# Layer 1's Gram matrices and weight products at the start of a two-layer decoder, layer 0's feed forward in the second part

## The chip, the cores and the metric

The kernel is one program on one core of a Trainium2 chip. The core has five engines that run their own instruction streams: TensorE (PE, matmuls, with weight loads shown as PEld), VectorE (DVE), ScalarE (ACT), GpSimd (POOL) and SyncE (SP, which here issues every DMA). The metric is device microseconds of one execution, the median of several runs. Before the change it is 2391.16 us (three runs, 2387.3 to 2392.27).

## What is computed

The input is 64 sequences of 64 tokens with 256 features, 4096 tokens in all, and a context of the same shape. Six blocks follow one another, each adding to x what it makes of the layer norm of x:

```
x = x + L0_attn(ln(x))          # 16 query heads of 128, 4 key/value heads, layer norm of q and k, rotary, causal
x = x + L0_xattn(ln(x), ctx)    # 8 channels a head; softmax over the 256 features of ctx; no weights
x = x + L0_ffn(ln(x))           # base 256x256, plus the rank-16 correction of the one expert (of 8) that the router picks
x = x + L1_attn(ln(x))          # 16 heads of 16, one key/value head, causal
x = x + L1_xattn(ln(x), ctx)    # 16 heads of 128; q and k with an RMS norm over all 2048 features; output 2048 -> 256
x = x + L1_ffn(ln(x))           # 704 wide, weights and activations quantized to 8 bits
```

Layer 1's cross attention needs two things of its weights alone. The RMS norm of x @ q_w + q_b over 2048 features is a quadratic form in x, so the kernel computes the Gram matrix of [q_w, q_b] (256 x 257, a sum over 2048 features), and the same for ki. And the value and output weights of each head are multiplied into one 256 x 256 matrix a head (the weight products).

## The kernel before

Tokens go in 16 groups of 256. A group's first part (attention a0, cross attention x0 and feed forward f0 of layer 0) ends with a store of x to DRAM ("mid"); its second part (a1, x1, f1 of layer 1) begins with the load. All sixteen first parts come before most of the second parts, as the weights of layer 0 and of layer 1 don't fit beside each other: a pool of 67 buffers of 2 KB a partition ("k2") holds 20 pieces of layer 0's weights and later 32 pieces of layer 1's.

Matmuls in full precision are made of three 16-bit matmuls (high x high, high x low, low x high), in the helper mm3 (lines 412 to 414); some are plain fp32.

No loop runs in the order in which it is written. Each step (a few instructions on one engine) is an Op with an estimated cost, the buffers it reads and writes, an earliest start (tmin) and a due time. A planner (Sched.plan) runs once when the program is built: it takes, again and again, the step that can start first; among steps that can start within EPS ns of each other it takes the one with the earliest due time. What it decides is each engine's instruction order, which the chip then follows strictly, with semaphores for the dependences. The due time is the group's base (PACE), plus the step's place in its group, plus a constant for each kind of step (the table LEAD). At most five groups are in flight (WINDOW). PSUM has eight banks (class "B"), which all stages share.

Setup work has no group. Layer 0's weights are loaded, centred, scaled by a power of two and split into two 16-bit parts (split_weight, lines 475 to 531). The scale of the context (ctx_scale) and layer 0's remaining setups follow with earliest starts of 30 to 70 us, among them l0_ffn_setup and l1_attn_setup. Layer 1's cross attention setup (l1_xattn_setup, line 1426) and feed forward setup have an earliest start of 150 us and more. In it:

- gram_setup (line 1326), once for q and once for ki: eight loads of 128 x 2 x 257 fp32; for each load and each half h of the 256 rows two fp32 matmuls into a fresh PSUM bank g_ps (line 1343), for h = 0 also one-column matmuls that sum the squares of the bias (line 1345), and an addition of the bank to an SBUF tile g_G on DVE (lines 1350 to 1354). STEP[0] = 15 us lie between the earliest starts of two loads.
- value_out_setup (line 1375): eight pairs of loads n_v and n_o, 32 fp32 matmuls into n_ps (line 1392), a copy and a sum of squares on ACT (lines 1395 and 426), a store to DRAM (line 1398); then, when the largest value is known, the products are read again, scaled, split (w_hl) and stored.

l1_xattn_load (line 1484) brings layer 1's prepared weights into k2 buffers. The first three weights wait for the attention of group 14, the other five for that of group 15.

l0_ffn (line 1108): a layer norm, a 16-bit split and a DMA transpose (to_T, line 556); for each half of the group six matmuls of 392 columns into f_ps, a routing chain of small DVE operations (lines 1129 to 1134), a transpose hm_ps, a copy hT, a fp32 matmul f0o_ps (line 1143) and two additions to x (lines 1136 and 1144).

Cross attention of layer 0 works with matmuls on quarters of PE's array (xs_ps line 1009, xt_ps line 1043, xo_ps line 1059), the row maximum on DVE (xmx, line 1016) and the exponential on ACT (line 1050). In layer 1's cross attention the value matrices (vn_ps, line 1511) are the largest single use of PE.

## Time and profile before

| what | value |
|---|---|
| median of 3 runs | 2391.16 us |
| the profiled execution's own time | 2390.41 us |
| its span, first to last instruction | 2388.5 us |
| PE busy | 2169.8 us (91%) |
| weight loads | 1701.9 us (71%) |
| DVE busy | 1948.4 us (82%) |
| ACT busy | 1516.3 us (63%) |
| POOL busy | 1630.4 us (68%) |
| mean granted PE clock | 0.961 |
| moved by DMA | 220.83 MB, 92 GB/s |

The profile is one execution. Busy time is the time in which an engine had at least one instruction running; matmuls overlap each other, so a sum of single durations is larger than the busy time. The page cuts the span into 40 slices of 60 us. "fill" below is busy time divided by the length of a stretch. Idle time of an engine says something about the end only where that engine sets the pace.

### The profile page before, as it was taken

What the parts mean: (1) busy time and instruction counts of PE and PEld (TensorE: products, weight loads), DVE (VectorE), ACT (ScalarE), POOL (GpSimd) and SP (SyncE); (2) the same over time, 40 slices, a digit from 0 to 9 for tenths busy, and PEclk for the clock granted to TensorE, in tenths of its full rate; (3) what the DMA queues carried; (4) which work ended last, traced back from release to release, by engine and by line L of the source; (5) the groups of instructions that cost most, each with busy time, mean ns of one, the idle gap of its engine ahead of it and who ended that gap; (6) DMA issues with size and microseconds to landing.
All of it is one profiled execution on the core that took longest, in us unless ns stands there. A gap on an engine that the chain in (4) does not pass through costs nothing. (4 is left out here: it accounts for less than half of the span.)

```text
span 2388.5 us, 69732 instructions
## 1 busy us (share of the span) xinstructions
PE 2169.8 (91%) x28232; PEld 1701.9 (71%) x28232; DVE 1948.4 (82%) x4532; ACT 1516.3 (63%) x2843; POOL 1630.4 (68%) x1572
## 2 busy tenths in 40 slices
PE   3499999888999898898878999999999999999996
PEld 2387666655566565665544779898999898899995
DVE  7768788898797889898988867887888888888767
ACT  6475666877878676777557565565556565566542
POOL 5899668777787577767645466767777666666632
PEclk9699999999999998999977999999999999999997
DMA  5243234444355333433464353343444334444321
GB/s 182 74 88 91 59 83 107 125 129 103 87 136 136 108 92 83 129 97 80 111 158 108 57 118 72 76 80 73 86 82 80 76 76 81 81 86 77 59 42 28
DMA packets 484323, 220.83 MB, mean 92 GB/s; under 512 B 340568, under 2 KB 463384, under 8 KB 484000
## 3 DMA queue, kind: packets, MB, share of 16 engines
q1 hardware_dynamic: 484000, 216.37, 39.9%
q8 instruction: 222, 3.64, 0.6%
q14 instruction: 101, 0.83, 0.1%
HBM read 89.06 MB, written 34.64 MB: 52 GB/s over the span
## 5 line engine op out<-in xcount | busy, mean ns | idle before, releaser
L1050 ACT ACTIVATE xpt<-xt_ps,xes 128x512 f32<-128x512 f32 x512 | 313.2, 698 | 75.5 <-PE xt_ps L1043 71.7
L1511 PE MATMUL vn_ps<-x1wn,cTs 128*64 128x256 f16 x6144 | 354.1, 274 | 0.0
L1511 PEld LDWEIGHTS <-cTs 128*64 128x64 f16 x6144 | 332.1, 110 | 8.4 <-issue 6.2
L1016 DVE TENSOR_REDUCE xmx<-xs_ps 128x2 f32<-128x512 f32 x512 | 317.2, 679 | 18.1 <-PE xs_ps L1009 17.4
L1518 DVE SCALAR_TENSOR_TENSOR vn<-vn_ps,vn 128x512 f16<-128x512 f32 x256 | 174.5, 684 | 96.9 <-ACT vn L1516 96.4
L1516 ACT ACTIVATE vn<-vn_ps 128x512 f16<-128x512 f32 x256 | 151.9, 595 | 159.3 <-PE vn_ps L1511 157.5
L604 POOL TENSOR_TENSOR s<-s,sm_mx 128x1024 f32<-128x1024 f32 x96 | 184.7, 1924 | 78.8 <-DVE sm_mx L603 71.4
L633 POOL TENSOR_TENSOR phl<-s,phl 128x512 f16<-128x512 f32 x192 | 223.6, 1176 | 12.3 <-ACT phl L632 10.3
L630 POOL TENSOR_TENSOR s<-s,sm_sm 128x512 f32<-128x512 f32 x192 | 199.5, 1056 | 4.7 <-POOL sm_sm L623 0.3
L1059 PE MATMUL xo_ps<-xpt,xve 128*32 128x256 f32 x2048 | 165.0, 414 | 7.1 <-DVE s L1291 4.9
L815 POOL TENSOR_TENSOR qu<-qu,sw 128x512 f32<-128x512 f32 x128 | 165.5, 1304 | 2.0
L813 POOL TENSOR_TENSOR sw<-sw,rp0s 128x512 f32<-128x512 f32 x128 | 165.3, 1304 | 2.2 <-ACT sq L811 1.6
L810 ACT COPY sw<-q_ps 64x512 f32<-64x512 f32 x256 | 148.0, 580 | 28.1 <-PE q_ps L414 18.8
L632 ACT CAST phl<-s 128x512 f16<-128x512 f32 x192 | 118.2, 622 | 73.7 <-POOL s L630 70.8
L1761 POOL TENSOR_TENSOR gu<-gu 128x704 f32<-128x704 f32 x32 | 55.0, 1721 | 138.2 <-ACT sig L1759 129.9
L1620 ACT ACTIVATE k<-qk_ps,x1kb 128x256 f32<-128x256 f32 x242 | 101.4, 471 | 72.6 <-PE qk_ps L414 67.3
L412 PE MATMUL q_ps<-xT,l0w 128*128 128x256 f16 x512 | 139.8, 273 | 3.7 <-ACT sw L810 1.8
L412 PE MATMUL acc<-l0w,ohl 128*128 128x256 f16 x512 | 141.7, 277 | 0.6 <-ACT sw L810 0.2
L413 PE MATMUL acc<-l0w,ohl 128*128 128x256 f16 x512 | 141.4, 276 | 0.0
L414 PE MATMUL acc<-l0w,ohl 128*128 128x256 f16 x512 | 141.3, 276 | 0.0
L412 PE MATMUL qk_ps<-cTs,x1wki 128*128 128x256 f16 x512 | 140.3, 274 | 0.0
L412 PE MATMUL qk_ps<-xT,x1wq 128*128 128x256 f16 x512 | 139.7, 273 | 0.2 <-DVE xmx L1016 0.2
(414 smaller groups left out, 6666.4 us busy)
## 6 DMA issues: line engine op xcount, KB each, us to landing
ovl<-hl_d SPq DMA_DIRECT2D x96, 128.0 KB
vx<-vt SPq DMA_DIRECT2D x64, 128.0 KB
ctx<-in_ctx_dram SPq DMA_DIRECT2D x32, 256.0 KB
hl_d<-hl SPq DMA_DIRECT2D x64, 128.0 KB
wd<-w_hl SPq DMA_DIRECT2D x32, 256.0 KB
q1st<-q_d SPq DMA_DIRECT2D x128, 64.0 KB
xt<-in_x_dram SPq DMA_DIRECT2D x16, 256.0 KB
ctx_a<-in_ctx_dram SPq DMA_DIRECT2D x8, 512.0 KB
```

The lines of the kernel that those rows point to most:

```text
L412: nc.tensor.matmul(out, lh, rh, start=(st and i == 0), stop=False, **kw)
L604: s.o("POOL", 1900, [mx], [s1], lambda m, t: nc.gpsimd.tensor_tensor(t, t, bc(m, 2, 64), ALU.subtract))
L630: s.o("POOL", 1030, [sm], [s1.sub(j)], lambda m, t, h=h: nc.gpsimd.tensor_tensor(t[:, h], t[:, h], bc(m[:, h], 2, 64), ALU.mult))
L633: s.alt([("POOL", c_pool(482), lambda t, _, p, h=h: nc.gpsimd.tensor_tensor(pl(p, 1), t[:, h], pl(p, 0), ALU.subtract)), ("DVE", c_dves(51 ...
L813: s.o("POOL", 1225, [sg], [sw], lambda t, w: nc.gpsimd.tensor_tensor(v(w), v(w), bc(t, 1, 8), ALU.mult))
L815: ("POOL", 1225, lambda w, d: nc.gpsimd.tensor_tensor(view(d), view(d), w, ALU.add))], [sw], [dt])
L1016: nc.vector.tensor_reduce(m[:, h, bs % 4, :], p, AX.X, ALU.max))
L1050: nc.scalar.activation(t, p, AF.Exp, scale=a))
L1059: nc.tensor.matmul(o[32 * hh:32 * hh + 32, hs, :], v[:, n, a:a + 32], r[hh][:, n, :], start=(n == 0 and hs == 0), stop=(n == 1), skip_grou ...
L1511: nc.tensor.matmul(r[-1][64 * h:64 * h + 64, p, :], x[:, b // 2, a, k, t], w.part(r, c, 2 * (2 * p + h) + k), start=(n == 0), stop=(n == 5))
L1516: nc.scalar.activation(v(t), p, AF.Copy, scale=2.0 ** -15))
L1518: nc.vector.scalar_tensor_tensor(v(l), p, 2.0 ** -15, v(h), ALU.mult, ALU.subtract))
```

## The change

Six things change. The Gram matrices accumulate over all eight loads in two PSUM banks; of the second half of the rows only the 129 columns from the diagonal block on are computed, and the sums are copied out (and doubled) once at the end. The products are split off into value_out_products, and both Gram matrices and the products get an earliest start of 5 us with 3 us between loads. Layer 1's self attention setup is called with layer 1's other setups, at 150 us. Layer 0's feed forward becomes the first stage of the second part, so "mid" holds x before it. Layer 1's weights wait for the attention of groups 12, 12, 13, 14 and then 15. The planner's numbers are new: EPS, PEN, LEAD, SPACE, SHIFT, PACE, WINDOW, three costs of PE, HOLD (which puts off a step that changes PE's tiling), a table FINE that shifts single steps of a group, and DVE as an alternative for four memsets.

In the diff the rows of the tables LEAD and FINE are left out:

```diff
--- before.py
+++ after.py
@@ -34,7 +34,7 @@
 WARM = 0.375 * TICK
 LAT = 180
 SWITCH = 96
-HOLD = 0
+HOLD = 55
 DMA_NS = 2300
 SP_NS = 480
 TR_NS = 1240
@@ -224,6 +224,9 @@
             base = g * ii if ph == "a" else ng * PACE["a"][0] + (g - ng) * ii + SHIFT
             for o, t in zip(ops, memo[ph]):
                 o.due += base + t * stretch
+            for i, n, v in FINE[ph]:
+                for o in ops[i:i + n]:
+                    o.due += v
 
     def pe_run(self, st, c, duty):
 
@@ -930,7 +933,8 @@
     two = s.T("k4", [4, 8 * D], F16, name="xtwo")
     s.o("POOL", 1500, [], [two], lambda t: nc.gpsimd.memset(t, 2.0))
     for t in w.q + w.k:
-        s.o("POOL", 2000, [], [t], lambda t: nc.gpsimd.memset(t, 0.0))
+        s.alt([("POOL", 2000, lambda t: nc.gpsimd.memset(t, 0.0)),
+               ("DVE", 1130, lambda t: nc.vector.memset(t, 0.0))], [], [t])
     for t in w.k:
         s.o("SP", DMA_NS, [two], [t], lambda a, t: nc.sync.dma_start(t[3::32].rearrange("p a m -> p (a m)"), a))
 
@@ -1009,7 +1013,7 @@
                         nc.tensor.matmul(p[h][:, mc, :], part(q, h, bs)[:, 128 * mc:128 * mc + 128],
                                          part(k, h, bs), start=True, stop=True)
             s.space = sp
-            s.o("PE", 300, rows, ps, f, duty=0.85, tile=1)
+            s.o("PE", 345, rows, ps, f, duty=0.85, tile=1)
             s.space = None
             for h in range(4):
                 s.o("DVE", c_dve(512), [ps[h]], [mx.sub((bs, h))], lambda p, m, bs=bs, h=h:
@@ -1043,7 +1047,7 @@
                             nc.tensor.matmul(p[h][:, n, :], part(k, h, bs)[:, 128 * n:128 * n + 128],
                                              part(q, h, bs), start=True, stop=True)
                 s.space = sp
-                s.o("PE", 300, [Q.sub(r) for r in (0, 1, 2, ("m", j))] + [K], ps, f, duty=0.85, tile=1)
+                s.o("PE", 325, [Q.sub(r) for r in (0, 1, 2, ("m", j))] + [K], ps, f, duty=0.85, tile=1)
                 s.space = None
                 for h in range(4):
                     s.o("ACT", c_act(512, 1), [ps[h], w.es], [pt[h]], lambda p, a, t:
@@ -1059,7 +1063,7 @@
                             nc.tensor.matmul(o[32 * hh:32 * hh + 32, hs, :], v[:, n, a:a + 32],
                                              r[hh][:, n, :],
                                              start=(n == 0 and hs == 0), stop=(n == 1), skip_group_check=True)
-                s.o("PE", 975, [ve] + pts[hs], [po], f, duty=0.82, tile=2)
+                s.o("PE", 1010, [ve] + pts[hs], [po], f, duty=0.82, tile=2)
             so = s.T("k2", [128, 2, D], name="so")
             s.alt([("ACT", c_act(512), lambda p, t: nc.scalar.copy(t, p)),
                    ("DVE", c_dve(512), lambda p, t: nc.vector.tensor_copy(t, p))], [po], [so])
@@ -1332,36 +1336,31 @@
     g = s.T("k4", [128, 2, 257], name="g_G")
     s.o("POOL", 600, [], [g], lambda t: nc.gpsimd.memset(t, 0.0))
     w.bb = s.fixed(c.tile([128, 1], F32, name=f"bb_{name}"))
+
+    pa, pb = s.T("B", [128, 258], name="g_ps"), s.T("B", [128, 129], name="g_ps")
     for q in range(8):
         t = s.T("k4", [128, 2, 257], name="g_w")
         s.o("SP", DMA_NS + 1500, [], [t], lambda t, q=q: nc.sync.dma_start(t, src[:, 2 * q:2 * q + 2, :]))
-        for h in range(2):
-            ps = s.T("B", [128, 258], name="g_ps")
-
-            def f(t, p, q=q, h=h):
-                for k in range(2):
-                    nc.tensor.matmul(p[:, 0:257], t[:, k, 128 * h:128 * h + 128], t[:, k, :], start=(k == 0), stop=(k == 1))
-                for k in range(2 - 2 * h):
-                    nc.tensor.matmul(p[:, 257:258], t[:, k, 256:257].to_broadcast([128, 128]), t[:, k, 256:257],
-                                     start=(k == 0), stop=(k == 1))
-            s.o("PE", 1108, [t], [ps], f)
-
-            def f(p, g, bb, q=q, h=h):
-                nc.vector.tensor_tensor(g[:, h, :], g[:, h, :], p[:, 0:257], ALU.add)
-                if h == 0 and q == 0:
-                    nc.vector.tensor_copy(bb, p[:, 257:258])
-                elif h == 0:
-                    nc.vector.tensor_tensor(bb, bb, p[:, 257:258], ALU.add)
-            s.o("DVE", 410 - 70 * h, [ps], [g.sub(h)] + ([w.bb] if h == 0 else []),
-                (lambda p, g, bb, f=f: f(p, g, bb)) if h == 0 else (lambda p, g, f=f: f(p, g, None)))
-        s.tmin += STEP[0]
+
+        def f(t, a, b, q=q):
+            for k in range(2):
+                kw = dict(stop=(q == 7 and k == 1), skip_group_check=True)
+                st = q == 0 and k == 0
+                nc.tensor.matmul(a[:, 0:257], t[:, k, 0:128], t[:, k, :], start=st, **kw)
+                nc.tensor.matmul(b, t[:, k, 128:256], t[:, k, 128:257], start=st, **kw)
+                nc.tensor.matmul(a[:, 257:258], t[:, k, 256:257].to_broadcast([128, 128]), t[:, k, 256:257],
+                                 start=False, **kw)
+        s.o("PE", 1600, [t], [pa, pb], f)
+        s.tmin += STEP[2]
     am = s.T("sm", [128, 1], name="g_am")
 
-    def f(g, bb):
-        nc.vector.tensor_scalar(g[:, 0, 128:257], g[:, 0, 128:257], 2.0, None, ALU.mult)
-        nc.vector.tensor_scalar(g[:, 1, 256:257], g[:, 1, 256:257], 2.0, None, ALU.mult)
-        nc.vector.tensor_scalar(bb, bb, 1.0 / 2048, 1e-6, ALU.mult, ALU.add)
-    s.o("DVE", 360, [], [g, w.bb], f)
+    def f(a, b, g, bb):
+        nc.vector.tensor_copy(g[:, 0, 0:128], a[:, 0:128])
+        nc.vector.tensor_scalar(g[:, 0, 128:257], a[:, 128:257], 2.0, None, ALU.mult)
+        nc.vector.tensor_copy(g[:, 1, 128:256], b[:, 0:128])
+        nc.vector.tensor_scalar(g[:, 1, 256:257], b[:, 128:129], 2.0, None, ALU.mult)
+        nc.vector.tensor_scalar(bb, a[:, 257:258], 1.0 / 2048, 1e-6, ALU.mult, ALU.add)
+    s.o("DVE", 850, [pa, pb], [g, w.bb], f)
     square_sum(e, g, am, 514, lambda a: a)
     sc, w.un = pow2_scale(e, am, 14, name)
     w.w = s.fixed(c.tile([128, 2, 2, 257], F16, name=f"gw_{name}"))
@@ -1372,13 +1371,12 @@
     return w
 
 
-def value_out_setup(e, I):
-
+def value_out_products(e, I):
 
     nc, s = e.nc, e.s
     w = e.x1
-    nd = s.fixed(e.dx.tile([4096, D], F32, tag="x1nf", name="nf_d"))
-    am = s.T("sm", [128, 16], name="n_am")
+    nd = w.nd = s.fixed(e.dx.tile([4096, D], F32, tag="x1nf", name="nf_d"))
+    am = w.am = s.fixed(e.cst.tile([128, 16], F32, name="n_am"))
     hv = lambda n, q: I[n].rearrange("(h p) n -> p h n", p=128)[:, 2 * q:2 * q + 2, :]
     for q in range(8):
         v, o = (s.T("k2", [128, 2, D], name="n_" + n) for n in "vo")
@@ -1397,7 +1395,15 @@
             square_sum(e, nf, am.sub(k), 512, lambda a, k=k: a[:, k:k + 1])
             s.o("SP", DMA_NS + 1400, [nf], [nd.sub(k)], lambda t, d, k=k: nc.sync.dma_start(
                 d[D * k:D * k + D].rearrange("(c p) n -> p c n", p=128), t))
-        s.tmin += STEP[0]
+        s.tmin += STEP[2]
+
+
+def value_out_setup(e, I):
+
+
+    nc, s = e.nc, e.s
+    w = e.x1
+    nd, am = w.nd, w.am
     am1 = s.T("sm", [128, 1], name="n_am1")
     s.o("DVE", 75, [am], [am1], lambda a, b: nc.vector.tensor_reduce(b, a, AX.X, ALU.max))
     sc, un = pow2_scale(e, am1, 14, "x1n")
@@ -1432,8 +1438,12 @@
     w.bo, w.i2 = col("bo", 128), col("i2", S)
     s.o("SP", DMA_NS, [], [w.bo], lambda t: nc.sync.dma_start(t, I["bones"]))
     s.o("SP", DMA_NS, [], [w.i2], lambda t: nc.sync.dma_start(t, I["i2"]))
+    t0 = s.tmin
+    s.tmin = STEP[3]
     w.gq = gram_setup(e, I, "gram_q")
     w.gk = gram_setup(e, I, "gram_k")
+    value_out_products(e, I)
+    s.tmin = t0
 
     s.o("DVE", 80, [w.gq.un], [w.gq.us],
         lambda a, t: nc.vector.tensor_scalar(t, a, 1.0 / (2048 * XS), None, ALU.mult))
@@ -1485,7 +1495,7 @@
     nc, s = e.nc, e.s
     order = [("ki", 0), ("q", 0), ("n", 0), ("n", 1), ("ki", 1), ("q", 1), ("n", 2), ("n", 3)]
     for i, (d, u) in enumerate(e.x1.w[k] for k in order):
-        s.after = after[i > 2]
+        s.after = after[i]
         for k, t in enumerate(u.tiles):
             s.o("SP", DMA_NS + 1500, [d], [t], lambda d, u, k=k: nc.sync.dma_start(
                 u, d[:, k // 2, 1024 * (k % 2):1024 * (k % 2) + 1024]))
@@ -1828,55 +1838,82 @@
     e.ctx_sc, e.ctx_un = pow2_scale(e, a1, 10, "ctx")
 
 
-EPS = 41.41
-PEN = 182.83
+EPS = 40.9
+PEN = 155.97
 NQ = 1
 LEAD = {
...
 }
+FINE = dict(a=[
...
 FOLD = [False, True]
-SPACE = (7898, 3165)
+SPACE = (7294, 2944)
 BURST = 1
-SHIFT = 2276.53
+SHIFT = -5805.18
 START = (0, 3e3, 15e3, 22e3, 40e3, 3e3, 30e3, 36e3, 60e3, 70e3)
-PACE = dict(a=(77726.07, 2.1), b=(72833.37, 2.08))
-STEP = (15e3, 60e3)
-WINDOW = (5, 6)
+PACE = dict(a=(74702.12, 2.31), b=(65478.21, 1.96))
+STEP = (15e3, 60e3, 3e3, 5e3)
+WINDOW = (5, 5)
 COUNTS = dict(B=8, k4=6, k2=67, k1=6, sm=10, dram=4)
 SIZE = dict(k8=8192, k4=4096, k2=2048, k1=1024, sm=256)
 
@@ -1901,15 +1938,15 @@
     common_setup(e, I)
 
     e.ovl = s.fixed(e.cst.tile([128, 4096 + 4096 * NQ], F16, name="ovl"))
-    sa = [n for n in stages if n in ("a0", "x0", "f0")]
-    sb = [n for n in stages if n in ("a1", "x1", "f1")]
+    sa = [n for n in stages if n in ("a0", "x0")]
+    sb = [n for n in stages if n in ("f0", "a1", "x1", "f1")]
     if "a0" in sa:
         l0_attn_setup(e, I)
     s.tmin = START[6]
     ctx_scale(e, I, nt)
-    for nm, f in (("x0", l0_xattn_setup), ("f0", l0_ffn_setup), ("a1", l1_attn_setup)):
+    for nm, f in (("x0", l0_xattn_setup), ("f0", l0_ffn_setup)):
         if nm in sa + sb:
-            s.tmin = START[dict(x0=7, f0=8, a1=9)[nm]]
+            s.tmin = START[dict(x0=7, f0=8)[nm]]
             f(e, I)
     s.tmin = 0.0
     mid = {}
@@ -1939,6 +1976,8 @@
         if g == min(1, ng - 1) and sb:
             s.grp = ng - 0.5
             s.tmin = 150e3
+            if "a1" in sb:
+                l1_attn_setup(e, I)
             if "x1" in sb:
                 l1_xattn_setup(e, I)
             if "f1" in sb:
@@ -1949,7 +1988,7 @@
         if not sa and "x1" in sb:
             l1_xattn_setup(e, I)
         if "x1" in sb:
-            l1_xattn_load(e, [e.done.get(("a0", max(g, 0))) for g in (ng - 2, ng - 1)])
+            l1_xattn_load(e, [e.done.get(("a0", max(ng - k, 0))) for k in (4, 4, 3, 2, 1, 1, 1, 1)])
         if "f1" in sb:
             if not sa:
                 l1_ffn_prep(e, I)
```

## The prediction

> **What bounds the kernel now.** I read the page's table of slices first, then busy time by stage, then what TensorE (PE) waits for in each stage, then the rows of the work that the change touches.
>
> The page's 40 slices (60 us each; busy tenths, and the granted clock):
>
> ```profile
> PE   3499999888999898898878999999999999999996
> DVE  7768788898797889898988867887888888888767
> PEclk9699999999999998999977999999999999999997
> DMA  5243234444355333433464353343444334444321
> ```
>
> PE is a third busy in the first two slices, eight to nine tenths until slice 22, and full from slice 23 on but for the last. The same in numbers, by stage (PE, weight loads, DVE, ACT, POOL busy, clock, DMA share, GB/s):
>
> ```profile
> 0.00:120.00 120.00, 50.20 (x399) 36.05 (x400) 89.47 (x228) 63.24 (x125) 86.43 (x95) 0.80 0.42 128
> 120.00:420.00 300.00, 285.47 (x3152) 214.22 (x3149) 241.52 (x577) 198.57 (x353) 243.27 (x213) 0.99 0.37 85
> 420.00:1140.00 720.00, 652.34 (x7469) 443.85 (x7468) 624.56 (x1438) 541.61 (x983) 538.91 (x489) 0.97 0.43 109
> 1140.00:1380.00 240.00, 200.82 (x2293) 124.52 (x2292) 203.70 (x466) 145.49 (x283) 126.86 (x129) 0.86 0.46 105
> 1380.00:2280.00 900.00, 895.24 (x13676) 808.27 (x13676) 713.21 (x1653) 531.15 (x1041) 605.43 (x618) 1.00 0.41 80
> 2280.00:2388.50 108.50, 85.72 (x1258) 74.95 (x1252) 75.98 (x173) 36.21 (x64) 29.44 (x32) 0.88 0.18 33
> 120.00:1380.00 1260.00, 1138.63 (x12909) 782.59 (x12907) 1069.78 (x2479) 885.67 (x1617) 909.05 (x829) 0.96 0.42 103
> ```
>
> PE idles 218.7 us in all: 69.8 before 120 us, 121.4 from 120 to 1380 (fill 1138.63/1260 = 0.904), 4.8 from 1380 to 2280 (fill 0.9947), 22.8 in the tail. So the second part is set by PE alone; the first part is nearly set by it (DVE follows at 0.849, POOL 0.721, ACT 0.703); the start is a chain of weight preparation in which PE has nothing to do. In the first part no single wait owns the idle time. The top of PE's waits from 420 to 1140:
>
> ```profile
> PE mx_ps L1018 <- DVE xmx L1016: 5.5, 8, 1.2
> PE s_ps L911 <- POOL kf L889: 4.6, 2, 4.1
> PE xt_ps L1043 <- DVE s L913: 3.4, 3, 2.7
> ```
>
> The largest is 5.5 of 67.7 us: an order written out beforehand that doesn't fit everywhere. PE work taken out there should therefore shorten the stage at about its fill.
>
> **The change, part by part.** All durations are of the profiled execution: 2390.41 us, span 2388.5; the median of the runs is 2391.16, 0.75 more.
>
> The rows:
>
> ```profile
> L1343 PE MATMUL g_ps<-g_w x128: 377/381/484, 162.8 to 397.6; 128*128 128x257 f32 x128
> L1392 PE MATMUL n_ps<-n_o,n_v x64: 379/379/483, 653.1 to 763.3; 128*128 128x256 f32 x64
> L1114 POOL TENSOR_TENSOR xt<-xt,f0b 128x512 f32<-128x512 f32 x16 | 20.9, 1307 | 23.0 <-DVE xh L547 22.5 <-PE ss_t L870 0.6
> L1143 PE MATMUL f0o_ps<-f0bw,hT 128*128 128x256 f32 x64 | 20.4, 416 | 0.4 <-ACT hT L1141 0.4
> ```
>
> *Gram matrices, old place.* The tile g_ps holds PE for 38.6 us in all between 163 and 398 us (192 records), and DVE for 14.1 us of additions, plus 1.1 us of doubling. All of it leaves the first part.
>
> *Gram matrices, new form.* A fp32 matmul of 256 columns costs 15.65/32 = 0.49 us (the products' row). Per load of two blocks there were four wide matmuls and two of one column, 38.6/16 = 2.41 us. Now two wide ones are 129 columns: half of the 0.49 streams, but two weight loads of 0.19 still precede it, so each saves 0.11 to 0.24 us. Sixteen loads: 3.5 to 7.8 us, I take 5.6, so 33 us. DVE gets five operations for each matrix instead of 16 additions and more (some 1.5 us each).
>
> *Products* (value times output weights): PE 15.65 us and ACT 22.3 us (16 copies of 0.58, 16 squares of 0.63 and 0.19) leave 653 to 768 us.
>
> *Where both go.* The first due time is 5 us, one load every 3 us, so some 5 to 80 us. PE needs 33 + 15.7 = 49 us more before 120 us, against 69.8 idle. That is the cover. If it were gone, 49/0.904 = 54 us come back. Two PSUM banks of eight are held through each matrix, and PE's queue now holds matmuls that wait for a load, with group 0's projections behind them in line.
>
> *What the start pays.* SP issues 16 Gram loads (0.55 us each), 16 of the products' loads and 16 stores (0.39 each), past the loads of layer 0's second weights, the context's and the transposes of group 0. That is 8.4 MB in and 4.2 out. DMA is saturated only at first:
>
> ```profile
> 0.00:20.00 20.00, 0.80 (x2) 0.50 (x2) 12.83 (x49) 6.96 (x18) 9.36 (x25) 1.00 0.85 281
> 60.00:80.00 20.00, 7.38 (x28) 3.18 (x28) 13.51 (x35) 15.23 (x29) 17.09 (x15) 0.54 0.38 120
> ```
>
> At 350 GB/s, the rate of the busiest slices there, 8.4 MB are 24 us. That is the upper end of the delay if every load stands ahead of one that layer 0 waits for. PE's own clock sets a similar end: from 60 to 120 us it had 0.60 of its clock, and 49 us of full-clock work at 0.60 are 81 us against 69.8 idle, 12 too many. The lower end is a gain: layer 1's attention setup leaves the start (ACT 3 us, DVE about 6, its loads), and PE's 26.3 us from 60 to 120 would be 16 at full clock, so at most 10 us earlier. Range -10 to +25, taken +8, nearer the middle, since the saturated 18 us come before most of the new loads.
>
> The Trainium skill, "TensorE: Matmul & The Clock Gate", section "Loop structure matters more than you think", speaks against this place: matmuls that each wait for a transfer let PE's clock fall to half. The 0.54 of the row above agrees. By the rule 49 us become 98, 28 more than the idle time, and the total would be 20 us above mine.
>
> *Layer 1's attention setup* moves into the first part: four bias records (1.0 us) and three scale reductions (0.8 each), 3.4 us of PE; its ACT and DVE work lies beside PE.
>
> *Layer 0's feed forward.* PE: projections 37.7, corrections 20.4, transposes 8.9, together 66.9 us, 4.2 a group. In undisturbed stretches at full clock a group takes 2.16 + 1.17 + 0.55 = 3.9. DVE 5.9 us a group (per half 0.155 + 0.225 + 0.162 + 0.216 + 0.283 + 0.474 + 0.476; layer norm 2.0), POOL 3.4, ACT 1.1, one DMA transpose. Fifteen of sixteen lie before 1380 us, so 62.7 us of PE leave the first part and 15 x 3.9 = 58.5 enter the second. There a group takes 64 us with DVE at 0.792; with 3.9 and 5.9 more, DVE is at (50.4 + 5.9)/67.5 = 0.83. PE stays the bound.
>
> *First part:* 1138.63 - 38.6 - 15.65 - 62.7 + 3.4 = 1025.1 us of PE, at 0.904 1134.4: 125.6 less. With DVE instead, 1069.78 - 15.1 - 89 + 5 = 970.7 at 0.849: 1143, 117 less; the two agree.
>
> "Perfetto Trace Analysis" of the skill, "Identifying the Most-Contended Engine", says that matmul busy time is a poor measure and weight-load busy time a better one. Here weight loads fill 0.62 from 420 to 1140 and 0.90 from 1380 to 2280; so by the rule the first part isn't PE's, DVE's sum applies, and the total is 9 us above mine.
>
> *Second part:* 58.5/0.9947 = 58.8 more.
>
> *New order* (all the leads, the fine shifts, the 55 ns against changing PE's tiling, earlier gates for layer 1's weights, memsets that DVE may do). No row prices it. Ends: the first part reaches the fill of 120 to 420 us (0.9516), 57 us less; or falls to that of 1140 to 1380 (0.837), 90 more. I take nothing, since removed and new order are of the same make, and keep the ends.
>
> Sum: 2390.41 - 125.6 + 58.8 + 8 = 2331.6, so **2332 us**.
>
> **The rivals.**
> - *The order tightens too.* The first part runs at 0.9516: 2332 - 57 = 2275. For it: 120 to 420 us ran so with the same stages. Against: Gram work was the filler there, and it is gone.
> - *The second part loses its fill* (slower). Feed forward puts a layer norm, a transpose by DMA and three rounds between PE and DVE ahead of each group's attention, while 32 of the 67 2-KB buffers hold layer 1's weights. If PE's fill there falls to the 0.906 of 420 to 1140, 953.7 us of PE take 1053 instead of 959: 94 more, 2426. It decides from a fill of 0.937 on. Against: PE's waits from 1380 to 2280 sum to 4.3 us, each group brings 60 us of other PE work.
> - *Not first after all.* The loads slip behind layer 0's and the 49 us run among its matmuls: 1073.8/0.904 = 1188, 72 less, so 2390.4 - 72 + 58.8 = 2377, and with the 8 us of delay 2385. For it: one SP queue issues all loads in order.
>
> **How the numbers follow.** Forecast 0.56, tighter order 0.21, second part 0.14, not first 0.09. Faster by over 0.2% (about what a measurement of this kernel can tell from no change, below 2386.4): 0.56 + 0.21 + 0.05 = 0.82; within 0.2%: 0.04 of the last case; slower: 0.14. The range 2270 to 2395 reaches to the tighter order below; above it holds the late start (+17), some loss in the second part, and the case "not first".
>
> **What would show it.** Right: g_ps and n_ps rows before about 100 us, PE near 95 us busy in the first 120; the first part done some 115 us earlier; the second part's PE still above 0.98 full, 67 to 68 us a group. Wrong: first projections of group 0 later by over 25 us; PE waits for feed forward's transpose or for DVE among the first five of the second part; g_ps after 150 us.

## The result, and the profile after

The changed kernel takes 2409.54 us (median of 4 runs, 2404.19 to 2410.84) against 2391.72 of the kernel before on the same chip: ratio 1.0074, 95% interval 1.0053 to 1.0094. It is slower by 0.74%, where 2332 us had been forecast. The profiled execution took 2404.19 us, with a span of 2402.4. The median is 5.35 us above it, so the traces show 14 of the 18 us. In what follows a ratio is always to the kernel before, measured in the same session; a number of us for it is that share of 2391.

The slices of the changed kernel, to lay beside those shown before:

```profile
PE   7897977988888889989779999999999999999995
DVE  7678878888798888788778589888888889988866
PEclk9998998999999989999879999999999999999997
DMA  7744533343343323243433443343454443453411
```

The first two slices went from 3 and 4 tenths of PE to 7 and 8: the Gram matrices and products lie there now. From slice 4 to slice 7 PE is *less* full than before (7 9 7 7 instead of 9 9 9 9). PE is full from slice 22 on instead of 23, and the span is longer. By stage (PE, weight loads, DVE, ACT, POOL busy, each with its count; clock, DMA share, GB/s):

```profile
0.00:120.00 120.00, 93.74 (x759) 77.38 (x760) 79.75 (x231) 86.05 (x186) 81.82 (x94) 0.97 0.77 223
120.00:420.00 300.00, 242.74 (x2649) 171.61 (x2647) 241.16 (x535) 194.11 (x350) 251.24 (x218) 0.91 0.42 108
420.00:1140.00 720.00, 640.95 (x7683) 437.40 (x7686) 607.31 (x1294) 519.62 (x918) 512.98 (x447) 0.96 0.36 89
1140.00:1380.00 240.00, 202.94 (x2526) 134.66 (x2520) 174.80 (x420) 150.52 (x288) 112.91 (x119) 0.90 0.40 95
1380.00:2280.00 900.00, 887.72 (x13220) 788.13 (x13218) 788.40 (x1808) 500.86 (x1022) 638.31 (x665) 1.00 0.43 78
2280.00:2402.40 122.40, 97.65 (x1414) 86.76 (x1410) 81.75 (x194) 44.42 (x83) 38.98 (x44) 0.89 0.19 39
120.00:1380.00 1260.00, 1086.63 (x12849) 743.67 (x12849) 1023.27 (x2246) 864.24 (x1554) 877.13 (x783) 0.94 0.38 95
```

Read the second row against that of before: 242.74 us of PE instead of 285.47. Gram matrices and feed forward had 46 us there by the rows of their tiles; 43 us of PE's busy time are gone with them, and nothing came in their place; PE idles instead. Its granted clock there is 0.91 instead of 0.99; no run separates what that costs from the idle time. From 120 to 1380 us the fill fell from 0.904 to 0.862. From 1380 to 2280 it is 0.986 instead of 0.9947, with DVE up from 713 to 788 us.

The rows of the moved work:

```profile
L1349 PE MATMUL g_ps<-g_w x64: 380/382/797, 13.0 to 64.5; 128*128 128x257 f32 x64
L1390 PE MATMUL n_ps<-n_o,n_v x64: 379/379/634, 69.8 to 104.0; 128*128 128x256 f32 x64
L1118 POOL TENSOR_TENSOR xt<-xt,f0b 128x512 f32<-128x512 f32 x16 | 20.6, 1286 | 3.3 <-PE xs_ps L1013 2.0 <-DVE xh L550 1.3
L1147 PE MATMUL f0o_ps<-f0bw,hT 128*128 128x256 f32 x64 | 19.3, 385 | 0.1
```

Both kinds of products are done by 104 us. Where did the time go? Some points of the trace tell it, each the end of the addition on DVE that puts a block's result onto x (for a0 L687 before and L690 after, for x1 L1538 and L1548):

| end of, us | before | after | difference |
|---|---|---|---|
| a0 of group 0 | 152 | 152 | 0 |
| a0 of group 3 | 336 | 374 | +38 |
| a0 of group 7 | 671 | 660 | -11 |
| a0 of group 15 | 1246 | 1187 | -59 |
| x1 of group 0 | 1460 | 1406 | -54 |
| x1 of group 15 | 2359 | 2370 | +11 |
| span | 2388.5 | 2402.4 | +14 |

The first part ends 54 us earlier, not 117.6 (the forecast's 125.6 less 8). The second part takes 65 us more (964 from first to last x1, 899 before), where 58.8 were forecast; a group takes 67.8 us instead of 63.7 (medians of the 15 steps between the ends of x1). The tail adds 3: -54 + 65 + 3 = 14.

The same marks split the time into PE's busy and idle share. From 120 us to the end of x1 of group 0, PE is busy 1218.0 us of 1339.5 before and 1112.5 of 1285.9 after: 105.5 us of its work are gone, and 52 of them came back as idle time. From there to the end of x1 of group 15 it is busy 891.1 us of 899.1 before and 949.9 of 964.4 after: 58.8 us more work and 6.5 more idle.

In the first part PE's waits are still many and small. From 120 to 420 and from 420 to 1140 us (waiting line and what it waits for: us in total, times, longest), the head of each list:

```profile
PE mx_ps L1022 <- DVE xmx L1020: 11.1, 2, 10.9
PE po L670 <- DVE xmx L1020: 7.7, 1, 7.7
```

```profile
PE ss L862 <- ACT sq L814: 5.8, 5, 2.3
PE xo_ps L1063 <- ACT xpt L1054: 5.7, 5, 2.5
PE q_ps L415 <- DVE y L1084: 4.9, 1, 4.9
```

Two of them, in the first list, are large: 10.9 and 7.7 us, both behind DVE. DVE's own timeline at the place of the longer one shows what held it up:

```profile
311.31 8.93 DVE L526 SCALAR_TENSOR_TENSOR w_hl<-w_x1ki,sc_x1ki,w_hl 128x512 f16<-128x512 f32 x4
320.17 1.21 DVE L624 TENSOR_REDUCE sm_sm<-s 128x16 f32<-128x1024 f32 x1
321.30 2.47 DVE L1020 TENSOR_REDUCE xmx<-xs_ps 128x2 f32<-128x512 f32 x4
```

Four splits of layer 1's key weights stand ahead of the maxima that PE needs. The splits of layer 1's key and query weights lay at 428 to 616 us before. They moved forward to 218 to 400 us, as the program's sixteen Gram loads with earliest starts 15 us apart no longer stand ahead of them: an effect of the change that the forecast had not listed.

### The profile page after: what moved, and what is told of

Same layout as the page of the kernel before. It is cut to its first block, busy times and chain, and to the rows that moved or that the text cites. A ratio compares the mean times of both kernels' runs of the same rounds, so it can differ in the third digit from the quotient of the medians.

```text
span 2402.4 us, 69638 instructions
## 1 busy us (share of the span) xinstructions
PE 2165.7 (90%) x28232; PEld 1696.0 (71%) x28232; DVE 1973.2 (82%) x4478; ACT 1495.6 (62%) x2842; POOL 1636.2 (68%) x1583
## 4 chain that ended last, share of the span: by engine, by line
PE 48%; DVE 14%; ACT 6%; DMA 5%; POOL 5%; issue 3%; SPq 1%; POOLq 0%; ACTq 0%; DVEq 0%
PE vn_ps L1521 10%; PE qk_ps L415 4%; PE qk_ps L416 3%; PE qk_ps L417 3%; PE acc L1544 3%; PE xo_ps L1063 3%; DVE xmx L1020 3%; PE gu_ps L1764 2%; ACT sw L813 2%; DMA xT<-xhl 2%; PE s_ps L1642 2%; PE acc L415 1%; DMA hqT<-hq 1%; PE s_ps L914 1%; PE gy_ps L1561 1%
## 5 line engine op out<-in xcount | busy, mean ns | idle before, releaser
L1521 PEld LDWEIGHTS <-cTs 128*64 128x64 f16 x6144 | 330.0, 110 | 11.3 <-issue 10.3
L607 POOL TENSOR_TENSOR s<-s,sm_mx 128x1024 f32<-128x1024 f32 x96 | 190.3, 1984 | 114.6 <-DVE sm_mx L606 107.0
L1063 PE MATMUL xo_ps<-xpt,xve 128*32 128x256 f32 x2048 | 158.0, 412 | 10.1 <-ACT xpt L1054 8.1
L415 PE MATMUL q_ps<-xT,l0w 128*128 128x256 f16 x512 | 141.7, 277 | 13.8 <-DVE y L1084 4.9
L416 PE MATMUL q_ps<-xT,l0w 128*128 128x256 f16 x512 | 141.6, 277 | 0.0
L417 PE MATMUL q_ps<-xT,l0w 128*128 128x256 f16 x512 | 141.5, 276 | 0.0
L417 PE MATMUL acc<-l0w,ohl 128*128 128x256 f16 x512 | 139.7, 273 | 2.0 <-DVE ohl L677 2.0
L415 PE MATMUL acc<-l0w,ohl 128*128 128x256 f16 x512 | 140.2, 274 | 1.3 <-DVE xmx L1020 1.3
L415 PE MATMUL qk_ps<-xT,x1wq 128*128 128x256 f16 x512 | 140.5, 274 | 0.0
L416 PE MATMUL qk_ps<-xT,x1wq 128*128 128x256 f16 x512 | 140.3, 274 | 0.0
```

The lines of the kernel that those rows point to most:

```text
L415: nc.tensor.matmul(out, lh, rh, start=(st and i == 0), stop=False, **kw)
L416: nc.tensor.matmul(out, lh, rl, start=False, stop=False, **kw)
L417: nc.tensor.matmul(out, ll, rh, start=False, stop=(i == n - 1), **kw)
L607: s.o("POOL", 1900, [mx], [s1], lambda m, t: nc.gpsimd.tensor_tensor(t, t, bc(m, 2, 64), ALU.subtract))
L1063: nc.tensor.matmul(o[32 * hh:32 * hh + 32, hs, :], v[:, n, a:a + 32], r[hh][:, n, :], start=(n == 0 and hs == 0), stop=(n == 1), skip_grou ...
L1521: nc.tensor.matmul(r[-1][64 * h:64 * h + 64, p, :], x[:, b // 2, a, k, t], w.part(r, c, 2 * (2 * p + h) + k), start=(n == 0), stop=(n == 5))
```

## The experiments

All kernels keep the written order of the kernel that they start from, so each shows what one piece of work costs at its place, in that order. What a new plan would make of the room is not in them. None of them undoes the change by halves with an order of its own; that was not tried.

### Does PE work pace the first part?

**The Gram matrices' PE work, at its old place.**

```
+  t = t.bitcast(BF16)[:, :, 1::2]                                         # t was fp32; upper halves
   for k in range(2): matmul(p[:, 0:257], t[:, k, ...], t[:, k, :], ...)   # the same matmuls
```

> The kernel before, every instruction and its place unchanged; only the Gram matmuls read the upper 16 bits of each fp32 number as bf16 instead of the whole number (the Gram matrices lose their lower bits). By the rows a 256-column matmul of 16-bit operands takes 0.11 us where the fp32 one takes 0.49, so about 28 of the 38.6 us of PE leave the stretch from 163 to 398 us. The prediction's step (PE work taken out of the first part shortens it at its fill): 28/0.95 = 29 us less, 2361, ratio 0.988. Rival (the Gram work lay in time that PE had to spare): 0 to 7 us less, ratio 0.997 to 1.000.

Measured: ratio 1.0005, 0.9994 to 1.0015. The wide matmuls went from 0.381 to 0.279 us, the time that g_ps holds PE from 38.6 to 11.6, and PE's busy time from 120 to 420 us from 285.47 to 268.00:

```profile
120.00:420.00 300.00, 268.00 (x3105) 193.66 (x3105) 245.51 (x592) 204.35 (x362) 247.93 (x218) 0.98 0.36 85
```

Nothing was gained. The PE time of this work had cost nothing in this order.

**Feed forward's PE work, at its old place.**

```
-  mm3(nc, p[:, 0:392], ...)                        # three products of 392 columns
+  matmul(p[:, 0:(392, 8, 8)[i % 3]], ...)          # the corrections on 8 columns; f0o_ps on bf16 halves
```

> The kernel before, order unchanged; in layer 0's feed forward the two corrections for low parts are done on 8 of 392 columns and the experts' output matmul on the upper 16 bits of its fp32 operands: about 11 + 17 = 28 us of PE work less, spread over the first part from 303 to 1415 us. The prediction's step: 28/0.904 = 31 us less, ratio 0.987. Rival (the first part gives back half or less): 0 to 15 us less, ratio 0.994 to 1.000.

Measured: 1.0002, 0.9991 to 1.0013. Again nothing, for 30 us in the rows of feed forward (f_ps, hm_ps and f0o_ps: 66.9 to 36.9 us). PE's busy time over the whole span fell by 20, from 2169.8 to 2150.1 us.

**Feed forward's DVE work, at its old place.**

```
-  scalar_tensor_tensor(x[:, j, :], p[:, 0:256], u, x[:, j, :], ...)       # both updates of x
+  scalar_tensor_tensor(x[:, j, 0:8], p[:, 0:8], u, x[:, j, 0:8], ...)     # and bn_stats on 8 columns in f0
```

> The kernel before, with DVE work of layer 0's feed forward cut by about 26 us and its PE work left whole: the two updates of xt (L1137, L1145) and the layer norm statistics (L537, feed forward alone) work on 8 of 256 columns (the other columns keep their old value). Sizes from the rows of before: 64 updates of 0.475 us and 32 statistics of 0.413 us, each left with an estimated 0.16 to 0.2. Theory A (layer 0's cross attention and self attention are held by the chain over DVE, POOL and ACT, so that feed forward takes DVE time from it): -10 to -25 us, ratio 0.990 to 0.996. Rival (the first part has spare time on DVE as it has on PE, and only the order and the latencies of the chain set it): -5 to +2 us, ratio 0.998 to 1.001.

Measured: 0.9995, 0.9983 to 1.0008. DVE's busy time from 120 to 1380 us fell from 1069.78 to 1048.57; the time did not move. The theory that DVE's load from feed forward holds the chain falls here, as PE's did.

**PE work on layer 0's own chain.**

```
-  mm3(nc, p[:, c, :]..., [...])                                # query and key projections
+  matmul(..., x[...][:, :, 0:(128, n, 128)[i % 3]], ...)       # n = 4 in a0: second product on 2 x 4 columns
```

> The kernel before, with PE work of layer 0's own chain cut: in the query and key projections of its self attention the second of three products (high part of the weight by low part of x) works on 8 of 256 columns (the rest of that correction is left out). 640 matmuls of 0.273 us, each left with about 0.166 us (the shortest in b_f0_thin): 68 us of PE less, all within 0 to 1246 us. The prediction's step (PE work taken from the first part shortens it at the fill of 0.904): -75 us, ratio 0.969. Theory A (PE is not what paces the first part; only the latency of each projection shortens, 1.3 us for each of 80 steps if none of it is hidden): -5 to -30 us, ratio 0.987 to 0.998.

Measured: 1.0011, 0.9996 to 1.0026. Here PE's busy time fell by less than the 68 us that I had worked out from durations: from 120 to 1380 us it is 1105.15, 33.5 less. Matmuls overlap: before, one of 0.273 us is followed by the next after 0.109; now the shortened one is followed after 0.026, so each saves 0.083 us. But 33.5 us taken from the very steps that the other engines wait for gave nothing either; the prediction's step would have given 37, and Theory A at least 5.

**All of it together.** The edits of b_gram_thin, b_f0_thin and b_f0_dve, and the products on bf16 halves:

```
-  matmul(p[:, c, :], v[:, h, ...], o[:, h, :], ...)
+  matmul(p[:, c, :], v.bitcast(BF16)[:, :, 1::2][:, h, ...], o.bitcast(BF16)[:, :, 1::2][:, h, :], ...)
```

> The kernel before, with all thinnings of the work that the change takes out of the first part put together: the Gram products on the bf16 upper halves (b_gram_thin, 27 us of PE), the products of the value and output weights on the bf16 upper halves as well (64 matmuls of 0.385 us, to about 0.28: 7 us of PE), feed forward's corrections on 8 columns and its second product on bf16 (b_f0_thin, 28.7 us of PE), and feed forward's DVE updates and statistics on 8 columns (b_f0_dve, 21 us of DVE as measured). What is left out is low parts of these products and the updates of the other columns. The prediction's step (fill 0.904): 63 us of PE less, -70 us, ratio 0.971. Theory A (this work lies in spare time of PE and DVE, jointly as well as singly; the order and the chain through the engines set the time): -12 to +2 us, ratio 0.995 to 1.001. Rival (PE and DVE take turns as the bound, so that only both together show it): -25 to -60 us, ratio 0.975 to 0.99.

Measured: 0.9941, 0.9927 to 0.9956: 14 us less. This is between the expectation of Theory A and that of the rival, nearer the first. By the rows of g_ps, n_ps and feed forward 68 us of PE are gone (the expectation's 63 counts 28.7 for feed forward and 7 for the products, where the rows give 30 and 10), and PE's busy time over the whole span fell by 47.5 (2169.8 to 2122.3), DVE's by 24 (1948.4 to 1924.3). Together they have a price of about a fifth of the two busy times; charged to PE alone it is 0.2 for each us of the rows or 0.3 for each of busy time, where the prediction charged 1.1.

```profile
120.00:1380.00 1260.00, 1104.01 (x12922) 748.38 (x12921) 1052.24 (x2488) 894.25 (x1631) 920.85 (x838) 0.95 0.42 104
```

### What does the first part respond to?

**DVE work of layer 0's cross attention.**

```
-  tensor_reduce(m[...], p, AX.X, ALU.max)
+  tensor_reduce(m[...], p[:, :, 0:128], AX.X, ALU.max)
```

> The kernel before, with DVE work of layer 0's cross attention cut: the row maximum (L1016) looks at the first 128 of 256 columns of each tile (so the subtracted maximum is that of half the row). 512 reductions of 0.679 us, each left with an estimated 0.41 us (by the reductions of 512 and 1024 elements, 0.679 and 1.206 us): about 137 us of DVE less in the first part. Theory A (DVE paces the first part with its chain): -60 to -140 us, ratio 0.94 to 0.975. Rival (PE paces the first part, or the written order and latencies do, DVE being busy 0.85 of it): -30 to 0 us, ratio 0.987 to 1.000.

Measured: 0.9922, 0.9893 to 0.9952: 19 us for 512 reductions that went from 0.680 to 0.414 us, 136 us of DVE. The rival holds: a seventh.

**POOL work of the rotation.**

```
-  gpsimd.tensor_tensor(v(w), v(w), bc(t, 1, 8), ALU.mult)
+  gpsimd.tensor_tensor(v(w)[:, 0:1], v(w)[:, 0:1], bc(t, 1, 8)[:, 0:1], ALU.mult)   # and the sum on an eighth
```

> The kernel before, with POOL work on layer 0's self attention chain cut: the two elementwise steps of the rotation on POOL (L813, L815) work on an eighth of each tile (the rest stays unrotated). 320 instructions of 1.29 us, each left with an estimated 0.35 us: about 300 us of POOL less, all between 55 and 1155 us, and some 1.9 us less of latency at each of 160 steps. Theory A (the chain through the engines, with POOL the longest of its steps, sets the first part, not PE): -50 to -150 us, ratio 0.937 to 0.98. Rival (the written order of each engine with its spare time sets it, and work taken from any single engine moves little): -25 to 0 us, ratio 0.99 to 1.000. By the prediction's step (PE paces at its fill) nothing: 0.

Measured: 0.9869, 0.9854 to 0.9883: 31 us for 307 us of POOL (320 instructions that went from 1.30 to 0.33 us). A tenth; it is between the two expectations, just above the rival's end. POOL's busy time from 120 to 1380 us dropped from 909 to 639 us, and PE's fill only rose to 0.912:

```profile
120.00:1380.00 1260.00, 1149.48 (x13327) 795.34 (x13325) 1060.04 (x2521) 900.47 (x1649) 639.47 (x844) 0.97 0.44 105
```

**Both sets together** (the edits of b_rope and b_all).

> The kernel before, with b_rope and b_all together: 300 us of POOL, 63 us of PE and 21 us of DVE less. Singly they gave -31 and -14 us. Theory A (the written order with its latencies takes the spare time of every engine alike): additive, -40 to -50 us, ratio 0.979 to 0.983. The prediction's step, rescued (PE paces once the POOL chain is out of the way): -31 - 70 = about -100 us, ratio 0.958.

Measured: 0.9802, 0.9783 to 0.9821: 47 us, where the two singly gave 31 + 14 = 45. This is the additive expectation. PE does not become the bound when the POOL chain is short: from 120 to 1380 us it is busy 1122 of 1260 us.

**The rotation in the changed kernel** (the edit of b_rope).

> The changed kernel, with the POOL steps of layer 0's rotation cut to an eighth as in b_rope (the rest stays unrotated): about 300 us of POOL less in the first part. b_rope gave -31 us (1.3%). Theory A (the chain over the engines sets the first part in both kernels alike): -25 to -45 us, ratio 0.989 to 0.997. Rival (with Gram and feed forward gone the chain is all that is left, so that its links count for more): -60 to -120 us, ratio 0.957 to 0.982.

Measured: 0.9944, 0.9923 to 0.9966. Against the changed kernel's 1.0074 that is 1.3 points, 31 us, the same as before the change. So, within some 7 us, the chain weighs no more now that Gram and feed forward are gone.

### What does feed forward cost in the second part?

**Its PE work** (the edit of b_f0_thin in the changed kernel).

> The changed kernel, order unchanged, with the same saving in layer 0's feed forward, where it now lies in the second part: about 28 us of PE less. Both theories have PE pace the second part: 25 to 28 us less than the changed kernel, ratio to the kernel before 0.996 to 0.998. Under 14 us less would mean that the second part isn't PE's any more with feed forward in it.

Measured: 1.0028, 1.0012 to 1.0043; 0.46 points, 11 us below the changed kernel (to some 6 us either way), for 30 us of PE in the rows of feed forward (65.7 to 35.7). The expectation of 25 to 28 us is missed, and 11 lies under the 14 us below which it said that the second part is no longer PE's. Still, the same edit gave nothing in the first part.

**Its DVE work** (the edit of b_f0_dve in the changed kernel).

> The changed kernel, with only the DVE work of feed forward in the second part thinned (21 us: two updates of xt and the statistics on 8 columns; the other columns keep their old value), PE work whole. a_f0_thin gave -11 us for 30 us of PE, a_f0_both -26 us for both. Theory A (in the second part PE and DVE both have a price, and it adds up): -10 to -17 us, ratio 1.000 to 1.003. Rival (PE is the bound until it is thinned, so DVE alone brings nothing): 0 to -4 us, ratio 1.006 to 1.008.

Measured: 1.0076, 1.0050 to 1.0103: nothing.

**Both.**

> The changed kernel, with feed forward in the second part thinned on PE (as in a_f0_thin, 30 us) and on DVE (updates and statistics on 8 columns, 21 us) together. Theory A (the second part is paced by PE, and feed forward's DVE work there lies beside it): as a_f0_thin, ratio 1.000 to 1.003. Rival (in the second part DVE holds PE back where feed forward has been added): another 8 to 20 us off, ratio 0.994 to 0.999.

Measured: 0.9965, 0.9952 to 0.9978; 1.09 points, 26 us below the changed kernel. The expectation that DVE lies beside PE there is wrong, and so is that of a_f0_dve that the two prices add up: PE alone 11, DVE alone 0, both 26. The traces agree: from the end of x1 of group 0 to that of group 15 it is 964 us in the changed kernel, 958 with PE's part thinned, 964 with DVE's, 948 with both. So DVE's work costs nothing there as long as PE's is whole; once that is shorter, something else stands close behind. The waits of PE from 1380 to 2280 us point to what: in the changed kernel, then in a_f0_thin, then in a_f0_both, the first entry of the list is

```profile
PE f1o_ps L1799 <- DMA hqT<-hq: 6.6, 7, 1.9
```

```profile
PE f1o_ps L1799 <- DMA hqT<-hq: 16.3, 17, 2.0
```

```profile
PE f1o_ps L1799 <- DMA hqT<-hq: 11.3, 13, 1.6
```

Part of what a_f0_thin took from PE came back as a wait for the DMA transpose ahead of layer 1's second feed forward product; with DVE relieved as well it is shorter again. That DVE is what delays it is a reading of these rows, not a measurement by itself.

### Do the early products cost the start anything?

The Gram and product edits of b_all, in the changed kernel:

> The changed kernel, with the Gram products and the products of value and output weights at the start thinned on PE (bf16 upper halves; low parts left out): about 16 us of PE less between 13 and 104 us. The prediction's step that held by the trace (the start hides this work): 0 to -3 us, ratio 1.006 to 1.008. Rival (the early products push layer 0's first groups back): -8 to -16 us, ratio 1.001 to 1.004.

Measured: 1.0082, 1.0050 to 1.0113, with PE's busy time in the first 120 us down from 93.74 to 74.22. No gain; the start hides this PE work. The loads are whole in this run, so what they cost is not tested by it.

### Does layer 1's weight setup, now earlier, hold layer 0 up?

**Its POOL work.**

```
-  gpsimd.tensor_tensor(t[:, 0], t[:, 0], b, ALU.mult)
+  gpsimd.tensor_tensor(t[:, 0, 0:8], t[:, 0, 0:8], b[:, 0:8], ALU.mult)
```

> The changed kernel, order unchanged, with POOL's multiplication of layer 1's query and key weights by the norm's scales done on 8 of 512 columns (16 operations of 1.27 us between 183 and 371 us, where the kernel before had them from 410 to 596; 19 us of POOL less). Theory that this setup work, which moved forward into layer 0's first groups when the Gram steps no longer stood before it, is what holds them up: 10 to 20 us less than the changed kernel, ratio to the kernel before 1.000 to 1.003. Rival (it isn't): 0 to 4 us less, ratio 1.006 to 1.0074.

Measured: 1.0084, 1.0068 to 1.0100: nothing, for 16 multiplications that went from 1.28 to 0.21 us. POOL was the busiest engine from 120 to 420 us (251 of 300), and is down to 237.81 there; so this work on the busiest engine had no price in that stage either.

**Its DVE work, at the new place and at the old.**

```
-  scalar_tensor_tensor(lv(b), fl(t), a, hv(b0), ALU.mult, ALU.subtract)
+  memset(lv(b), 0.0) if spill else scalar_tensor_tensor(...)     # low parts of layer 1's q and k weights
```

> The changed kernel, order unchanged; the low parts of layer 1's query and key weights are set to zero instead of computed (16 DVE operations of 0.74 to 6.9 us between 218 and 400 us become short memsets; some 23 us of DVE less). Theory that this weight setup, which now lies in layer 0's first groups, holds them up through DVE: 10 to 25 us less than the changed kernel, ratio to the kernel before 0.997 to 1.003. Rival (it does not): 0 to 4 us less, ratio 1.006 to 1.008.

Measured: 1.0029, 1.0011 to 1.0047; 0.45 points, 11 us below the changed kernel. It looked like the cause.

> The kernel before, with the low parts of layer 1's cross attention query and key weights written as zero by a memset instead of the DVE scalar_tensor_tensor at L523 (the low parts of these weights are left out of the result); the same edit as in a_low0, but where the kernel before does this work (428 to 547 us). Theory A (the changed kernel pays for having this weight setup among layer 0's first groups, at 180 to 400 us): here the same edit gains little, 0 to -4 us, ratio 0.998 to 1.000. Rival (this DVE work costs the same at any place in the first part): about -11 us as in a_low0, ratio 0.995 to 0.996.

Measured: 0.9957, 0.9935 to 0.9978: 10 us less than the kernel before. DVE's time for these splits went from 16.8 to 4.4 us here, and from 24.1 to 4.4 in a_low0. Within the intervals (5 to 16 us here) the work costs the same at its old place, so its move explains none of the difference that these runs can see, and the theory that I had formed from the 10.9 us wait falls. It is a good example of a wait that is real and of a kernel that is slower, with no line between them.

## Why the prediction was wrong

**The step that failed** is the sentence under the first views: "PE work taken out there should therefore shorten the stage at about its fill." It priced 113.5 us of PE (1138.63 down to 1025.1) at 125.6 us. The first part gave 54, although the late start of 8 us was not paid: the work did go (105.5 us of busy time), but half of it came back as idle time, and the fill fell from 0.904 to 0.862 instead of holding. The runs show the price of that work at its place and in the old order: 0 for the 27 us of Gram, 0 for the 30 of feed forward, 0 for 33.5 on the chain itself, 14 for 68 us of PE's rows and the DVE work together. A fill of 0.904 had been read as "nearly set by it". It was a stage in which PE is not the bound, and DVE and POOL are not either by the cuts made on them; ACT, at a fill of 0.703, was not tried. Spread over the groups, cuts on PE, DVE and POOL each gave back between none and about a fifth of what was taken, and the prices of the two sets that were run singly and together added up (31 + 14 against 47). Only the weight splits on DVE paid more: 10 us for 12.4 in b_low0, 11 for 19.7 in a_low0. What remains as the pace is the order of the steps across the engines, with a few us of waiting at dozens of places; that is argued from what the cuts did not do, and no run tests it by itself. The views had hinted at it: the largest of PE's waits from 420 to 1140 us was 5.5 of 67.7 us. I read that as a blemish of a full engine.

The check by DVE (117 us at 0.849) failed for the same reason, and its agreement with PE's sum was worth nothing: both divided removed work by a fill. The Trainium skill, "Perfetto Trace Analysis", section "Identifying the Most-Contended Engine", prefers weight-load busy time to matmul busy time as a measure of PE. By it PE was at 0.62 there, which spoke against PE as the bound; that half was right. The conclusion that I drew from it, that DVE's sum applies, was not: b_xmx paid 19 us for 136.

**The start** was right. PE is 93.74 us busy in the first 120 (forecast: near 95), group 0's attention ends at 152 us in both kernels, and a_gram_thin gains nothing. The late start of 8 us did not come. The slow clock came only in patches: PE's clock over the first 120 us is 0.97, and after a wait of 3.60 us for a load the wide Gram matmul at 27.2 us took 0.775 us instead of 0.380, and after one of 3.00 us the products at 71.3 to 73.9 us took 0.634 instead of 0.379; from 30 us on the wide Gram matmuls are at 0.380 to 0.484. The skill's "TensorE: Matmul & The Clock Gate", section "Loop structure matters more than you think", expects the slow clock where a long wait for a transfer stands before every matmul; here group 0's projections lie between the loads. From 60 to 80 us, with the DMA queues at 0.99, PE had 0.91 of its clock:

```profile
60.00:80.00 20.00, 16.53 (x117) 13.49 (x115) 11.49 (x56) 14.05 (x31) 13.73 (x14) 0.91 0.99 277
```

It is more than the 0.54 of the same stretch before the change. PE was busier, 16.53 us of 20 instead of 7.38.

**The second part** was right in mechanism and close in size: 65 us instead of 58.8, 67.8 us a group (forecast 67 to 68). Part of that is luck. PE's busy time between the ends of x1 of groups 0 and 15 did grow by 58.8 us, but feed forward's rows hold only 47.4 of it (12 of 16 groups lie there, not 15); the rest is other work of layer 1 that came to lie between these marks. "PE stays the bound" holds as far as a_f0_dve goes. Its clearance was overrated: in a_f0_thin 30 us of PE gave 11, and a_f0_both shows DVE and the chain behind it close enough to take over. Of the signs of being wrong, a wait for DVE does stand among the first five of the second part, but with 0.7 us; and PE waits for feed forward's transpose once, 13.3 us at 1191 to 1205 us, in the handover between the parts:

```profile
PE f_ps L415 <- DMA xT<-xhl: 13.3, 1, 13.3
```

**The rivals.** None of the three came. The order did not tighten (0.862, not 0.9516), the second part kept its fill (0.986, where 0.937 had been given as the point of danger), and the products did come first. The missing rival was the plain one: that the first part pays little for work removed. At the price of b_all, 14 us for 68 us of PE's rows, the 113.5 us, which are a sum of such rows, are worth 23, and the sum is 2390.41 - 23 + 58.8 = 2426, slower. The kernel came out between, at 2404 to 2411.

**What stays open.** The first part ended 54 us earlier, over twice the 23 that the thinned runs lead one to expect. Whole steps went, with their transposes, waits and instructions on all engines, and not just a part of their work; and the planner's order is new. These runs cannot separate the two, nor say why the first part is 38 us late at group 3 and 59 early at group 15, since every run keeps an order as it was. No run points to a version that beats the kernel before without leaving work out.

## What to carry to other kernels

A high busy share does not make an engine the bound. Here a fill of 0.9, with its idle time spread over dozens of small waits, was the mark of a stage that PE did not set: work thinned there paid nothing to a fifth, and work removed with a new plan about half. Work that entered the stage at a fill of 0.99 was paid in full (58.8 us of PE's busy time made it 65 us longer), though thinning 30 us of it there gave back only 11. So moving filler from the first kind of stage to the second lost here, where the sum of durations promised a gain. Thin a piece of work in place, without touching the order, before crediting its removal, and make the same cut in both kernels before calling a wait the cause.

## What the runs showed of the hardware

Single DVE instructions can stretch a great deal. The split at L526 has a median of 0.739 us, and one of eight took 6.946:

```profile
L526 DVE SCALAR_TENSOR_TENSOR w_hl<-w_x1ki,sc_x1ki,w_hl x8: 737/739/6946, 218.1 to 319.5; 128x512 f16<-128x512 f32 x8
```

POOL ran without a pause from before its start until 0.55 us before its end. In the kernel before, the split of layer 0's feed forward weights (f0w, 128x784) took 11.3 us, with POOL at work without a pause until 0.83 us before its end; in the changed kernel it took 1.44. In a_rope, where POOL's steps are short, the longest split of these key weights is 2.836 us. That POOL is the reason is not shown: in a_f0_dve, with POOL's work whole, the longest is 2.830.

A matmul's duration is not its price on PE. In b_l0_pe 640 matmuls fell from 0.273 us to 0.167 at the shortest, 68 us by durations. By starts each saved 0.083 us (0.109 to 0.026 until the next one), 53 us, and PE's busy time from 120 to 1380 us fell by 33.5.
